# Turning a spectrum for the row transform: 90 TensorE transposes, or VectorE's 32x32 blocks of overlapping row ranges

## The chip, the cores and the metric

The kernel runs on one core of a Trainium2 chip. The metric is the device time of one execution in microseconds (us), the median of several runs; lower is better. All arithmetic is fp32.

A core has engines that each work through a queue of their own, in order: TensorE (PE in the profile; PEld is its loading of weights), VectorE (DVE), ScalarE (ACT), GpSimd (POOL) and SyncE (SP, which here only starts DMA transfers). They wait for each other by semaphores. TensorE writes into PSUM, and what is needed again is copied from there into SBUF.

## The reference

The input x is 8 images of 8 channels of 256 x 256. A Fourier neural operator in 4 groups runs on the normalized image, then a 3x3 dilation follows. Cut to what matters:

```python
h = _gconv1x1(h, fc0_w, fc0_b)                 # 4 groups x 10 channels
for i in range(4):
    h1 = _spectral_conv(h, sp_w1[i], sp_w2[i]) # rfft2, keep 24 x 12 modes, mix 10x10 channels, irfft2
    h2 = _gconv1x1(h, w_w[i], w_b[i])
    h = h1 + h2
    if i < 3:
        h = _gswish(h, betas[i])
h = _gswish(_gconv1x1(h, fc1_w, fc1_b), betas[3])   # 4 x 128 hidden channels
return _gconv1x1(h, fc2_w, fc2_b)
...
x = x + conv(gn(x)); x = x + dilate3x3(gn(x))
```

Only 12 modes along the width and 24 along the height are kept, so the kernel does the transforms as matrix products: first along the width (256 columns to 12 complex modes), then along the rows (256 rows to 24 modes).

## The kernel before, in words

**Staging.** One image's state `h` (40 channels of 256 x 256) stays in SBUF for all four layers. Its free dimension is cut into 11 chunks (`NCH`); every chunk has two rows for each of 4 x 3 sets (`NQ` quarters and `NBLK` blocks). The 30 channel-and-block rows of a group or of a quarter, with two spare ones, lie in 32 partitions.

**A layer** (`layer`, L423) goes through the chunks. `burst` (L469) multiplies the state by the layer's weights (L479) and adds the inverse transform of the mixed spectrum (L482, which reads `zt`); ScalarE's Silu puts the result back into `h` (L488). In layers 0 to 2 the forward transform for the next layer is made at the same time: `turn` (L426) transposes the new state in 32x32 blocks on VectorE (L430), `transform` multiplies by the cosine table along the width (L447) and `gather` (L453) adds the four partial sums by a matrix of identities (L461) and copies the sum, the spectrum along the width, into `zt` (L464, L467). `zt` has the shape [128, 22 rows, 4, 32]: after the bursts have read their part of the old contents, the new ones take their place. Before the change, the 128 partitions are 4 groups x 32 modes, and the third index runs over the quarters.

**Between two layers** `spectrum_h` (L312) takes the transform along the rows. For this the row index must lie in the partitions, so `zt` is turned first: for each of 30 columns, TensorE transposes a [128 x 88] slice (22 rows x 4 quarters) into PSUM (L320), eight of them into one PSUM tile `p_at`, and a copy (L195 on VectorE, in the first image every other one L193 on ScalarE) puts it into `turned`. Then 48 matrix products (L332), which the profile counts as 96 instructions, contract the rows with the table `eh_f` into `p_b`; six small products put the result into `bt`. `mix` (L352) multiplies by the spectral weights with 6 products (L359) and 6 sums (L362) on VectorE, `p_f` (L378) folds the result, and `rows_of` (L397) makes the inverse transform along the rows (`p_g`, L404 or L409) and writes it to `zt`. `spectrum_h` runs for layers 1, 2 and 3 of each image, 24 times in all.

**The head of the previous image.** The two last convolutions (`head`, L607) are done for the previous image beside the layers of the current one, in 128 steps. A step has a `first` (L627: 4 products with 512 columns into two PSUM tiles, two Silus of 1024 elements on ScalarE, L629) and, in every other step, a `second` (L649: 8 products into one PSUM tile, then an addition on VectorE, L652 or L654). The output of the dilation of the image before that (`dilate`) is woven in as well. For the first image there is no previous one; the last image's head runs alone at the end.

**The order of the work** is written out by hand: the instructions stand on each engine's queue in the order in which the program emits them. The generators of the layers yield numbers; `step()` emits one head step for each full unit of the running sum, where a number counts with a factor `scale` so chosen that the 128 steps are used up by the image's end:

```python
else:
    loose += n
    share += n * scale if scale else 0
    while share >= 1.0:
        share -= 1.0
        step()
scale = scale or (STEPS - exact) / loose
```

A tuple such as `(1,)` in the bursts stands for an exact number of steps, and `"even"` and `"odd"` add one where the count calls for it.

**PSUM** is one pool of four buffers of two banks, handed round in order of emission (`ps_z`). A `first` takes two, a `second` one, `p_at`, `p_b`, `p_f`, `p_g` one each.

The functions that the diff touches, and what calls them, as they stand before:

Of the kernel before, what the change touches and what calls it, by code (L numbers as in the profile page):

```python
# [20 lines left out]
G = 4  # L21
WID = 10
# [10 lines left out]
NBLK = 3  # L33
NCH = 11
NQ = 4
# [9 lines left out]
def fno_dilate_kernel(ctx: ExitStack, tc: tile.TileContext, a: dict, out: bass.AP):  # L45
# [28 lines left out]
    def load(name, shape, eng=nc.gpsimd):  # L74
        t = const.tile(list(shape), F32, tag=f"c_{name}", name=f"c_{name}")
        eng.dma_start(t, a[name])
        return t
# [20 lines left out]
    fold = load("fold", (128, 3, 32))  # L98
    rowg = load("rowg", (128, NBLK, NQ, CS))
    binv = load("binv", (128, HW))  # L100
    eh_f = load("eh_f", (CS * NQ, 3, NBLK, 32))
    bias3 = load("bias3", (128, 1))
    w1 = load("w1", (128, NBLK, HID))
    w2 = load("w2", (128, G, 47))
# [203 lines left out]
    def spectrum_table(k, term):  # L308

        return 0 if k == term else (1 if k == 0 else 2)  # L310

    def spectrum_h(b, l, out_):  # L312

        rows = turned.rearrange("p t f -> p (t f)")[: CS * NQ, : NBLK * WID * 128]
        view = rows.rearrange("p (i g k) -> p i g k", g=G, k=32)
        for j0 in range(0, NBLK * WID, 8):
            n = min(8, NBLK * WID - j0)
            t = ps_z(f"p_at_{b}_{l}_{j0}")
            for i in range(n):
                nc.tensor.transpose(  # L320
                    t[: CS * NQ, i // 4, 128 * (i % 4) : 128 * (i % 4 + 1)],
                    zt[:, :, :, j0 + i].rearrange("p r j -> p (r j)"), ident)
            copy(
                j0 // 8, rows[:, 128 * j0 : 128 * (j0 + n)], t[: CS * NQ].rearrange("p u w -> p (u w)")[:, : 128 * n])
            yield 0.6
        p = ps_a(f"p_b_{b}_{l}")
        for k in range(2):
            for n in range(2 * NBLK):
                term, blk = n // NBLK, n % NBLK
                for q in range(4):  # L330
                    k0 = 12 * term + 3 * q
                    mm(p[part(q), 120 * k : 120 * k + 120], eh_f[:, spectrum_table(k, term), blk, :],  # L332
                       view[:, WID * blk : WID * (blk + 1), :, k0 : k0 + 3],
                       start=n == 0, stop=n == 2 * NBLK - 1)
        bt = sb.tile([128, 2, 3, G, WID], F32, tag="B", bufs=1, name=f"B_{b}_{l}")
        s = io[:, 4 * l : 4 * l + 4]
        for part_ in range(2):
            for k in range(3):
                nc.vector.tensor_tensor(
                    bt[:, part_, k].rearrange("p g i -> p i g"),  # L340
                    p[:, 120 * part_ : 120 * part_ + 120].rearrange(
                        "p (i g k) -> p i g k", i=WID, g=G)[:, :, :, k],
                    s.unsqueeze(1).to_broadcast([128, WID, G]), ALU.mult,
                )
        out_["bt"] = bt
# [77 lines left out]
    def layer(b, l, out_, stored, side):  # L423
        group_in_f = l % 2 == 1

        def turn(c):  # L426

            dst = turned[:, c % 3].rearrange("p (s f x) -> p f s x", s=2, f=NQ)
            for i in range(2):
                nc.vector.transpose(  # L430
                    dst[:, 2 * i : 2 * i + 2], h[:, c, 2 * i : 2 * i + 2].rearrange("p f (s x) -> p f s x", s=2))

        def chunks_of(k):

            return sorted(range(2 * k, min(2 * k + 2, NCH)), key=lambda c: c % 3)

        def transform(k):


            cs = chunks_of(k)  # L440
            n, lo = len(cs), cs[0] % 3
            step = cs[-1] % 3 - lo if n == 2 else 1
            t = turned[:, lo : lo + step * (n - 1) + 1 : step].rearrange("p n (r v i) -> p n r v i", r=2 * NQ, v=8)
            pair = [ps_z(f"p_d_{b}_{l}_{k}_{i}") for i in range(2)]
            for v in range(8):
                for q in range(NQ):
                    mm(pair[q // 2][part(v % 4), q % 2, : 240 * n], fw8[part(q), v, :],  # L447
                       t[part(q), :, :, v, : NBLK * WID], start=v < 4, stop=v >= 4)
            e = turned[:, (2 * k + 1) % 3, : 960 * n].rearrange("p (q x) -> p q x", q=NQ)
            for i in range(2):  # L450
                copy_2(i, e[:, 2 * i : 2 * i + 2], pair[i][:, :, : 240 * n])

        def gather(k):  # L453

            cs = chunks_of(k)
            n = len(cs)
            e = turned[:, (2 * k + 1) % 3, : 960 * n].rearrange("p (q r f i) -> p q r f i", q=NQ, r=2 * n, f=NQ)
            p = ps_a(f"p_u_{b}_{l}_{k}")
            for g in range(G):
                m = e[:, g] if group_in_f else e[:, :, :, g].rearrange("p q r i -> p r q i")  # L460
                mm(p[part(g), : 240 * n], stack, m, start=True, stop=True)  # L461
            src = p[:, : 240 * n].rearrange("p (r j i) -> p r j i", r=2 * n, j=NQ)
            if cs == sorted(cs):
                nc.vector.tensor_copy(zt[:, 4 * k : 4 * k + 2 * n, :, : NBLK * WID], src)  # L464
            else:
                for i, c in enumerate(cs):
                    nc.vector.tensor_copy(zt[:, 2 * c : 2 * c + 2, :, : NBLK * WID], src[:, 2 * i : 2 * i + 2])  # L467

        def burst(c):  # L469
            pair = [ps_z(f"p_z_{b}_{l}_{c}_{i}") for i in range(2)]  # L470
            for f in range(NQ):
                for q in range(NQ):
                    o = pair[q // 2][part(f), q % 2, :]
                    if l == 0:
                        k = slice(32 * q, 32 * q + 6)
                        mm(o, wcn[k, :], h[k, c, f, :], start=True, stop=False)
                    else:
                        g = f if group_in_f else q
                        mm(o, wt[part(q), l, g, :], h[part(q), c, f, :], start=True, stop=False)  # L479
            for s in range(2):  # L480
                for q in range(NQ):
                    mm(pair[q // 2][:, q % 2, HW * s : HW * (s + 1)],  # L482
                       zt[part(q), 2 * c + s].rearrange("p f o -> p (f o)"), binv[part(q), :],
                       start=False, stop=s == 1)
            for i in range(2):
                dst = h[:, c, 2 * i : 2 * i + 2, :]
                if l < 3:
                    nc.scalar.activation(dst, pair[i], AF.Silu)  # L488
                else:
                    nc.scalar.activation(dst, pair[i], AF.Identity, bias=bias3)  # L490
            if l == 3:
                nc.sync.dma_start(stored[c], h[:, c].rearrange("p f w -> p (f w)"))

        def read_x(c):
            for g in range(G):
                nc.sync.dma_start(
                    h[32 * g : 32 * g + 6, c].rearrange("p f w -> p (f w)"), a["xp"][b, c, g])

        if l == 0:
            for c in range(NCH):  # L500
                read_x(c)
            wcn = sb.tile([128, 32], F32, tag="wcn", bufs=1, name=f"wcn_{b}")
            nc.vector.tensor_scalar(wcn, wc, out_["mr"][:, 1:2], None, ALU.mult)
        if l == 3:
            room = 0.0
            yield "odd"
            for c in range(NCH):
                burst(c)
                room += SIDE
                while room > 0.0:  # L510
                    room -= next(side, SIDE)
                yield (LAST,)
            return
        yield "even"
        for c in range(NCH):
            k = c // 2
            if c % 2 == 0:
                burst(c)
                yield (1,)
                turn(c)  # L520
                if k > 0:
                    transform(k - 1)
            else:
                burst(c)
                if k > 0:
                    gather(k - 1)
                yield (1,)
                turn(c)
        out_["sw"] = [load_sw(l + 1, 0), load_sw(l + 1, 1)]
        yield 1  # L530
        gather(k - 1)
        transform(k)
        yield 2
        gather(k)
        yield 1

# [251 lines left out]
def _tables():  # L788
# [17 lines left out]

    eh = np.where(real[None, ..., None], rows[:, row_of], 0.0).reshape(3, NBLK, NQ, CS, 32)
    eh = eh.transpose(2, 3, 0, 1, 4)

    line = np.linspace(0.0, 1.0, HW).astype(f32)  # L810

# [25 lines left out]
    for j, v in enumerate(planes):  # L837
# [8 lines left out]
    edge[:, 0], edge[:, 1] = np.where(top, -BIG, BIG), np.where(bottom, -BIG, BIG)  # L846
    edge[:, 2], edge[:, 3] = np.where(top, PAD, -BIG), np.where(bottom, PAD, -BIG)
    tables = {
        "fw": fw, "fw8": fw8, "stack": np.tile(np.eye(32), (4, 1)), "eh0": eh0, "eh_f": eh.transpose(1, 0, 2, 3, 4).reshape(CS * NQ, 3, NBLK, 32),
        "rowg": rowg.reshape(128, NBLK, NQ, CS),  # L850
        "fold": fold.reshape(128, 3, 32), "binv": binv.reshape(128, HW),
        "xe": xe.reshape(128, 6, G, 5), "grp": grp, "edge": edge,
# [68 lines left out]
```

## Time and profile before

| | before |
|---|---|
| time, median of 3 runs | 4109.72 us (4108.55 to 4111.58) |
| span of the profiled execution | 4109.4 us |
| mean granted clock of TensorE | 0.979 |
| TensorE busy | 93% |
| ScalarE busy | 70% |
| VectorE busy | 60% |
| head: L629 on ScalarE / L627 and L649 on TensorE | 1961.8 / 1201.7 and 996.9 us |
| L430, transposes of the state on VectorE | 622.9 us |

How to read it: a group of instructions is named by its line, engine and operation, then by what it writes and reads with the partitions and elements; after the count come the busy time of the group in us and the mean duration of one instruction in ns, then the idle time of the engine just before them and what ended it. For TensorE the busy time counts overlapping instructions once, so that busy time divided by count gives the pace, and the mean the time from start to end of one. Slices are fortieths of the span; a digit is the busy share in tenths. The first image takes up the time until about 400 us, the last head alone the time from about 3730 us.

### The profile page before, as it was taken

How to read it: one execution, taken by the hardware profiler on the slowest of the kernel's cores; microseconds unless marked ns; L12 is line 12 of the kernel's file. 1: busy time of each engine (PE TensorE's matmuls, PEld its weight loads, DVE VectorE, ACT ScalarE, POOL GpSimd, SP SyncE). 2: the span in 40 equal slices, each digit the busy share in tenths (PEclk: the TensorE clock that was granted, in tenths of full speed). 3: DMA queues.
4: the chain of work that ended last, by engine and by line, in shares of the span. 5: the costliest groups of instructions: out<-in, count | busy, mean ns of one | idle time of the engine just before them, and what ended most of it. 6: DMA issues, size and time to landing. Idle time of an engine off the chain costs nothing. (4 is left out here: it accounts for less than half of the span.)

```text
span 4109.4 us, 120095 instructions
## 1 busy us (share of the span) xinstructions
PE 3822.8 (93%) x54250; PEld 1529.8 (37%) x54250; DVE 2472.1 (60%) x3529; ACT 2860.1 (70%) x2997; POOL 117.0 (3%) x202
## 2 busy tenths in 40 slices
PE   5768999999999999999999999999999999999997
PEld 2434433333333343433333334343433433333222
DVE  6665565556566566665666666655676666663533
ACT  3436676776767777676777766777676776668887
POOL 1000000000000000000000000000000000000000
PEclk8988999999999999999999999999999999999998
DMA  2014111422125211261113511144121531215311
GB/s 83 14 46 157 56 42 33 163 88 64 57 75 175 64 57 57 83 195 43 58 57 108 175 47 48 49 145 136 55 58 47 169 101 59 61 47 191 94 52 48
DMA packets 113991, 345.09 MB, mean 84 GB/s; under 512 B 15772, under 2 KB 18396, under 8 KB 98057
## 3 DMA queue, kind: packets, MB, share of 16 engines
q1 hardware_dynamic: 95288, 276.33, 21.5%
q0 software_dynamic: 18192, 61.08, 4.5%
q8 instruction: 427, 7.00, 0.7%
q14 instruction: 84, 0.68, 0.1%
HBM read 213.36 MB, written 123.74 MB: 82 GB/s over the span
## 5 line engine op out<-in xcount | busy, mean ns | idle before, releaser
L629 ACT ACTIVATE act<-p_fc 128x1024 f32<-128x1024 f32 x2048 | 1961.8, 1026 | 735.1 <-PE p_fc L627 730.8
L627 PE MATMUL p_fc<-hs,c_w 32*128 32x512 f32 x8192 | 1201.7, 632 | 14.6 <-issue 8.3
L649 PE MATMUL p_fc<-act,c_w 128*32 128x512 f32 x8192 | 996.9, 603 | 47.1 <-ACT act L629 35.5
L627 PEld LDWEIGHTS p_fc<-hs,c_w 32*128 32x128 f32 x8192 | 398.3, 183 | 690.0 <-ACT act L629 270.4
L488 ACT ACTIVATE h<-p_z 128x1024 f32<-128x1024 f32 x528 | 511.7, 1021 | 189.1 <-PE p_z L482 188.6
L430 DVE STREAM_TRANSPOSE turned<-h 128x1024 f32<-128x1024 f32 x528 | 622.9, 1219 | 20.2 <-ACT h L488 19.9
L654 DVE TENSOR_TENSOR y<-p_fc,y 128x512 f32<-128x512 f32 x392 | 271.0, 691 | 543.0 <-PE p_fc L649 541.6
L649 PEld LDWEIGHTS p_fc<-act,c_w 128*32 128x32 f32 x8192 | 222.1, 110 | 636.2 <-issue 349.3
L482 PE MATMUL p_z<-c_binv,zt 32*128 32x256 f32 x5632 | 411.1, 405 | 0.9 <-ACT zt L193 0.9
L479 PE MATMUL p_z<-h,c_wt 32*32 32x512 f32 x8448 | 371.3, 602 | 6.7 <-DVE y L652 3.8
L482 PEld LDWEIGHTS p_z<-c_binv,zt 32*128 32x128 f32 x5632 | 261.3, 186 | 306.2 <-issue 289.1
L447 PE MATMUL p_d<-turned,c_fw 32*32 32x480 f32 (+1 forms) x9216 | 310.6, 541 | 12.5 <-DVE turned L430 12.5
L195 DVE COPY zt<-p_g 128x264 f32<-128x264 f32 x300 | 162.4, 629 | 169.5 <-PE p_g L409 94.0
L490 ACT ACTIVATE h<-p_z,c_bias 128x1024 f32<-128x1024 f32 x176 | 186.5, 1110 | 48.1 <-PE p_z L482 47.8
L199 ACT ACTIVATE turned<-p_d 128x960 f32<-128x960 f32 x144 | 130.0, 903 | 97.4 <-PE p_d L447 97.4
L447 PEld LDWEIGHTS p_d<-turned,c_fw 32*32 32x32 f32 x9216 | 121.8, 103 | 188.9 <-issue 151.3
L362 DVE TENSOR_REDUCE S<-turned 128x80 f32<-128x800 f32 x192 | 188.9, 984 | 5.0
L359 DVE TENSOR_TENSOR turned<-t,B 128x800 f32<-128x800 f32 x192 | 188.5, 982 | 0.9 <-DMA t<-in_spw 0.9
L461 PE MATMUL p_u<-turned,c_stack 128*32 128x480 f32 (+1 forms) x1152 | 137.9, 548 | 45.1 <-DVE turned L201 43.0
L479 PEld LDWEIGHTS p_z<-h,c_wt 32*32 32x32 f32 x8448 | 94.3, 103 | 205.8 <-ACT act L629 68.3
L201 DVE COPY turned<-p_d 128x960 f32<-128x960 f32 x144 | 152.1, 1057 | 30.3 <-PE p_d L447 30.1
L195 DVE COPY turned<-p_at 88x1024 f32<-88x1024 f32 x90 | 101.7, 1155 | 75.8 <-PE p_at L320 70.7
(172 smaller groups left out, 2134.7 us busy)
## 6 DMA issues: line engine op xcount, KB each, us to landing
stored<-h SPq DMA_DIRECT2D x88, 1024.0 KB
hs<-stored SPq DMA_DIRECT2D x352, 256.0 KB
t<-in_spw SPq DMA_DIRECT2D x96, 400.0 KB
yin<-y_rows POOLq DMA_DIRECT2D x56, 512.0 KB, 4.8
h<-in_xp SPq DMA_DIRECT2D x352, 48.0 KB
turned<-in_x SPq DMA_DIRECT2D x16, 1024.0 KB
y<-in_x SPq DMA_DIRECT2D x56, 256.0 KB
y_rows<-y POOLq DMA_DIRECT2D x56, 256.0 KB, 2.3
```

Of the source, the lines that this page charges most:

```text
L195: nc.vector.tensor_copy(dst, src)
L359: nc.vector.tensor_tensor(pr, sw[k], bt[:, k2, k].unsqueeze(2).to_broadcast([128, G, 2 * WID, WID]), ALU.mult)
L362: nc.vector.tensor_reduce(s[k2][:, k].rearrange("p g s o -> p (g s o)"), pr.rearrange("p g m i -> p (g m) i"), AX.X, ALU.add,)
L430: nc.vector.transpose(dst[:, 2 * i : 2 * i + 2], h[:, c, 2 * i : 2 * i + 2].rearrange("p f (s x) -> p f s x", s=2))
L447: mm(pair[q // 2][part(v % 4), q % 2, : 240 * n], fw8[part(q), v, :], t[part(q), :, :, v, : NBLK * WID], start=v < 4, stop=v >= 4)
L479: mm(o, wt[part(q), l, g, :], h[part(q), c, f, :], start=True, stop=False)
L482: mm(pair[q // 2][:, q % 2, HW * s : HW * (s + 1)], zt[part(q), 2 * c + s].rearrange("p f o -> p (f o)"), binv[part(q), :], start=False, s ...
L488: nc.scalar.activation(dst, pair[i], AF.Silu)
L627: mm(pair[g // 2][:, g % 2, :], w1[part(g), blk, :], hs[k][part(g), :], start=True, stop=True)
L629: nc.scalar.activation(act[:, 2 * i : 2 * i + 2, :], pair[i], AF.Silu)
L649: mm(acc[part(g), :], w2[:, g, 15 - rb - i : 47 - rb - i], act[:, g, :], start=i == 0, stop=i == 1)
L654: nc.vector.tensor_tensor(y, sums, y, ALU.add)
```

## The change

The transform along the rows gets its turned spectrum from VectorE. VectorE can transpose 32x32 blocks, each within 32 partitions. For this `gather` now writes `zt` so that the 128 partitions are 4 quarters x 32 modes and the third index runs over the groups (it loops over the quarters in place of the groups). `spectrum_h` then transposes, in four instructions, one for each group, 30 blocks of 32 modes x 32 rows. A chunked quarter has only 22 rows, so a block takes rows 0 to 15 and rows 6 to 21 (`windows`): ten rows appear twice. The table `eh_f` has 128 rows in place of 88 and holds zeros for the second appearance. The matrix products into `p_b` keep their number and columns and contract 128 partitions. The PSUM tiles `p_at` and their copies are gone. In place of the four yields of 0.6 there are four of 1.2.

```diff
-    eh_f = load("eh_f", (CS * NQ, 3, NBLK, 32))
+    eh_f = load("eh_f", (128, 3, NBLK, 32))
...
+    def windows(g):
+
+        v = zt[:, 0:16, g, : NBLK * WID].rearrange("p r i -> p i r")
+        (pp, pn), (i0, i1), (r0, r1) = [tuple(x) for x in v.ap]
+        return bass.AP(v.tensor, v.offset, [[pp, pn], [i0, i1], [(CS - 16) * r0, 2], [r0, r1]])
+
     def spectrum_h(b, l, out_):
 
-        rows = turned.rearrange("p t f -> p (t f)")[: CS * NQ, : NBLK * WID * 128]
-        view = rows.rearrange("p (i g k) -> p i g k", g=G, k=32)
-        for j0 in range(0, NBLK * WID, 8):
-            n = min(8, NBLK * WID - j0)
-            t = ps_z(f"p_at_{b}_{l}_{j0}")
-            for i in range(n):
-                nc.tensor.transpose(
-                    t[: CS * NQ, i // 4, 128 * (i % 4) : 128 * (i % 4 + 1)],
-                    zt[:, :, :, j0 + i].rearrange("p r j -> p (r j)"), ident)
-            copy(
-                j0 // 8, rows[:, 128 * j0 : 128 * (j0 + n)], t[: CS * NQ].rearrange("p u w -> p (u w)")[:, : 128 * n])
-            yield 0.6
+        rows = turned.rearrange("p t f -> p (t f)")[:, : NBLK * WID * 128]
+        view = rows.rearrange("p (g i k) -> p i g k", g=G, k=32)
+        for g in range(G):
+
+            nc.vector.transpose(
+                rows[:, 960 * g : 960 * (g + 1)].rearrange("p (i r) -> p i r", r=32), windows(g))
+            yield 1.2
         p = ps_a(f"p_b_{b}_{l}")
...
-            for g in range(G):
-                m = e[:, g] if group_in_f else e[:, :, :, g].rearrange("p q r i -> p r q i")
+            for g in range(NQ):
+                m = e[:, :, :, g] if group_in_f else e[:, g].rearrange("p q r i -> p r q i")
                 mm(p[part(g), : 240 * n], stack, m, start=True, stop=True)
-            src = p[:, : 240 * n].rearrange("p (r j i) -> p r j i", r=2 * n, j=NQ)
+            src = p[:, : 240 * n].rearrange("p (r g i) -> p r g i", r=2 * n, g=G)
...
+    eh_f = np.zeros((NQ, 32, 3, NBLK, 32))
+    eh_f[:, :16], eh_f[:, 48 - CS :] = eh[:, :16], eh[:, 16:]
```

The title's 90 are the transposes of one image's three calls.

More of the change, by code (lines that the diff above doesn't have):

```diff
@@ L848, in _tables @@
     tables = {
-        "fw": fw, "fw8": fw8, "stack": np.tile(np.eye(32), (4, 1)), "eh0": eh0, "eh_f": eh.transpose(1, 0, 2, 3, 4).reshape(CS * NQ, 3, NBLK, 32),
+        "fw": fw, "fw8": fw8, "stack": np.tile(np.eye(32), (4, 1)), "eh0": eh0, "eh_f": eh_f.reshape(128, 3, NBLK, 32),
         "rowg": rowg.reshape(128, NBLK, NQ, CS),
```

## The prediction

> **What bounds the kernel now.** I read the page first, then the groups by line, the waits of TensorE, and the timeline of one place where the changed code runs. From the page:
>
> ```profile
> PE 3822.8 (93%) x54250; PEld 1529.8 (37%) x54250; DVE 2472.1 (60%) x3529; ACT 2860.1 (70%) x2997; POOL 117.0 (3%) x202
> ...
> PE   5768999999999999999999999999999999999997
> ```
>
> TensorE is busy in nine tenths or more of every slice between the first image (slices 1 to 4) and the end, and no other engine is over 70%. A busy TensorE can still hide waits, so I look at what the operations concerned cost:
>
> ```profile
> L430 DVE STREAM_TRANSPOSE turned<-h 128x1024 f32<-128x1024 f32 x528 | 622.9, 1219 | 20.2 <-ACT h L488 19.9
> ...
> L362 DVE TENSOR_REDUCE S<-turned 128x80 f32<-128x800 f32 x192 | 188.9, 984 | 5.0
> ...
> L195 DVE COPY turned<-p_at 88x1024 f32<-88x1024 f32 x90 | 101.7, 1155 | 75.8 <-PE p_at L320 70.7 <-ACT act L629 5.1
> L320 PE MATMUL p_at<-ident,zt 128*88 128x128 f32 x720 | 92.4, 278 | 1.6 <-DVE zt L464 1.6
> ...
> L332 PE MATMUL p_b<-turned,c_eh_f 88*32 88x120 f32 x2304 | 90.6, 293 | 3.2 <-DVE turned L195 3.2
> ...
> L195 DVE COPY turned<-p_xt 128x512 f32<-128x512 f32 x56 | 35.3, 684 | 41.1 <-PE p_xt L250 41.1
> ...
> L195 DVE COPY turned<-p_a 32x512 f32<-32x512 f32 x28 | 28.7, 1025 | 28.1 <-PE p_a L263 25.6 <-ACT turned L193 2.2
> ```
>
> The busy sum of L320 is 92.4 us: 3.85 us for each of the 24 calls of spectrum_h (8 images, 3 layers), 128 ns a transpose, although one lasts 278. They run back to back. The timeline of one interleaved call, start and duration first (lines of other engines left out):
>
> ```profile
> 2056.71 0.41 DVE L464 COPY zt<-p_u 128x240 f32<-128x240 f32 x1 [2.16 <-PE p_u L461]
> ...
> 2059.87 1.98 PE L320 MATMUL p_at<-ident,zt 128*88 128x128 f32 x16
> ...
> 2061.08 2.35 DVE L195 COPY turned<-p_at 88x1024 f32<-88x1024 f32 x2 [0.73 <-ACT act L629]
> ...
> 2068.98 3.12 PE L332 MATMUL p_b<-turned,c_eh_f 88*32 88x120 f32 x80 [0.35 <-DVE turned L195]
> ...
> 2074.95 2.01 PE L627 MATMUL p_fc<-hs,c_w 32*128 32x512 f32 x16
> 2075.09 0.69 DVE L654 TENSOR_TENSOR y<-p_fc,y 128x512 f32<-128x512 f32 x1 [0.28 <-PE p_fc L649]
> ...
> 2077.26 1.93 PE L649 MATMUL p_fc<-act,c_w 128*32 128x512 f32 x16 [0.30 <-ACT act L629]
> ```
>
> From 2056.9 to 2072.1 us (15.2 us) the windows give TensorE 14.81 busy, VectorE 6.88, ScalarE 7.64. So TensorE is what this stage lasts, with hardly a gap: the head steps of the previous image (first: 4 L627 matmuls, about 1.02 us of TensorE; second: L649, 1.92 us, then one VectorE add of 0.69) fill it between the transposes. In the mix after it a second and two firsts repeat every 4.17 us, of which 0.3 is TensorE waiting for ScalarE's Silu.
>
> **The Trainium skill.** "TensorE: Matmul & The Clock Gate", Part 4 (PE-mode transpose), says that a full transpose goes to PSUM and needs a copy after it, and that most of a transpose's recorded time is access latency; the trace agrees (278 ns recorded, 128 ns apart, and the copies L195). "Vector Engine (DVE) Microarchitecture Reference", section 3.8, says that the 32x32 transpose streams one element per cycle per lane; L430 shows 1219 ns for 1024 elements, 1.19 ns each with its start-up, and reads contiguously. "SBUF — State Buffer", Door 1 (the remark on cachelines), says that accesses which cross to a new 16-byte line each time pay a penalty. The new transposes read zt with 512 bytes between consecutive elements. No row of before has such a read on VectorE; strided writes do show a penalty (worked out below).
>
> **The change, part by part.**
>
> *Removed from TensorE:* 30 transposes per call, 3.85 us; per interleaved image 3 x 3.85 = 11.6 us. The p_b matmuls stay 96 of 120 columns; 128 rows in place of 88 and another order of strides I take as free, since runs of 3 elements are gathered in both. The four PSUM buffers of p_at go too.
>
> *VectorE:* three copies of 1.22 and one of 0.95 go (4.6 us), four transposes T of 960 elements come. Duration T, from both sides: at the rate of L430, (960/1024) x 1219 = 1.15 us. With the strided penalty: the copy of p_a (same 512 elements, written 64 bytes apart) takes 1025 against 684 ns for p_xt, 0.67 ns per element more, so T = 1.15 + 960 x 0.67 ns = 1.8 us. The upper bound is an access at half rate, about 1.15 + 1.0 = 2.15 us. I take 1.8: a read of the SBUF that touches a new line each time should be no cheaper than such a write. VectorE's total then rises by 24 x (7.2 - 4.6) = 62 us; at 60% busy the total costs nothing, but the place can.
>
> *Gather:* the loop over q in place of g exchanges which layers read e contiguously; the p_u matmuls take 1.01 us for 8 in either kind of layer, so nothing. The larger eh_f is loaded once.
>
> *Emission:* a call now yields 4 x 1.2 = 4.8 units instead of 2.4, so more of the previous image's 128 steps fall into it, and fewer elsewhere (the sum stays 128). The instruction order of the changed program gives, between the last p_u and p_b, 5, 6 and 6 firsts and 2, 3 and 3 seconds for the three layers, where before had 4, 3, 3 and 2, 2, 1. The mixes lose one or half a step each.
>
> *The wait that is left:* p_b must wait for the fourth T. Behind the T's in VectorE's queue stand the adds of the seconds, each of which waits for its L649 and releases a PSUM buffer. I walk through it with time 0 at the end of the last p_u, zt copied at 0.55, firsts and seconds at the pace 4.17 per pair:
> - first layer: T1 to 2.35; add and statistics of the second 3.05 to 4.45; T2, T3 to 8.05; add to 8.75; T4 to 10.55. TensorE has done its steps by about 9.4 (the last first waits for the buffer of that add). Wait: 1.2.
> - second layer: T1 2.35; add, statistics 4.45; T2 6.25; add about 7.8; T3, T4 to 11.4. TensorE is busy to about 12.4. Wait: 0.
> - third layer: add, statistics to 3.4; T1, T2 to 7.0; add 7.7; T3 9.5; add (its L649 ends at 10.3) to 11.05; T4 12.85, against 12.35. Wait: 0.5.
> That is about 1.8 us per image.
>
> *Lost besides:* the transposes filled the 0.27 us in which TensorE otherwise waits for ScalarE in each pair of steps; five pairs per image (those that stood among them) lose it: 1.3 us. In the mixes, with fewer steps, p_f now comes sooner after VectorE's last product; walking through the orders I find 0.9 us in one of the three mixes and little in the others: 1.0 us.
>
> *Net per interleaved image:* 11.6 - 1.8 - 1.3 - 1.0 = 7.5 us; seven such images: 52.5 us.
>
> *The first image* has no head steps beside it, so the chain is bare: zt copied at 119.73 us of the trace, p_b's main run at 123.95, 4.2 us. Now 4 x 1.8 + 0.1 = 7.3: 3.1 us longer, three times, 9.3 us slower.
>
> Sum: 4109.7 - 52.5 + 9.3 = 4066.5 us.
>
> **Rivals.**
> - *The strided read is free* (T = 1.15). No wait before p_b, 0.5 in the mixes: 7 x (11.6 - 1.3 - 0.5) = 68.6; first image + 0.3 to 0.5 each, 1.5. Time 4043. For it: the transposing array is said to sustain a cycle per element. Against it: the cost of strided writes.
> - *Slower transposes or more given back* (T = 2.15, waits 2.2 + 0 + 1.1 = 3.3, mixes 1.5): 7 x 5.5 = 38.5, first image 13.5: 4085. If mixes, p_g and p_u also return 5 us per image at T = 1.8, 7 x 3.5 - 9.3 = 15: 4094. For it: the mix keeps VectorE at 11.09 of 13.2 us. Against it: where before has the same order of steps ahead of p_f, waits at p_f are 0.7 us in 500.
> - *VectorE becomes the bound of the call, and it is slower.* It takes T near 3.2: the walks then end at 15.4, 15.4 and 17.6, waits 14.3 us per image, so 7 x (14.3 + 1.3 + 1.5 - 11.6) = 38 more, and 26 in the first image: 4174. For it: a long queue on an in-order engine with TensorE at its end. Against it: no strided row of before is over about 1.8 ns per element without start-up (p_g's copy: 629 ns for 264), where this needs 3.2.
> - *No change* needs T about 2.6 or a new hidden bound; ScalarE, at 70%, has room for steps that come 1% sooner.
>
> **How the numbers follow.** T = 1.8: 0.55; free stride: 0.22; slower or given back: 0.13; slower than before: 0.06; near no change: 0.04. The likeliest is 4066. The range goes from just under the free stride, 4037, to the larger give-back, 4095; what is left out is 0.1 to 0.2. Faster (under 4101.5): the first three cases less a part of the third's tail, 0.88; same 0.05; slower 0.07.
>
> **What would show it.** Right: L320 as a TensorE line gone (-92 us of busy TensorE), 96 new STREAM_TRANSPOSE with a mean near 1.8 us, p_b waiting for them 1 us in the first and third layers and none in the second, about 3 us more per call in the first image. A mean of 1.15 makes the time 4043; one over 2.6 makes the forecast wrong. If the mean is 1.8 and the gain still under 25 us, the fault lies in the redistribution of the head steps: then waits at p_f, p_g or p_u will have grown.

## The result, and the profile after

| | before | after |
|---|---|---|
| time, median | 4109.16 us (4 runs, 4108.55 to 4111.58) | 4048.69 us (4 runs, 4043.43 to 4052.02) |
| ratio to before, 95% interval | | 0.9851 [0.9834, 0.9868] |
| TensorE busy | 3822.8 us | 3734.7 us |
| VectorE busy | 2472.1 us | 2538.8 us |

The changed kernel is 60 us faster; 43 were forecast (4066, range 4037 to 4095). The profiled execution of after is the fastest of its four (span 4041.6). The lines of its page that answer to those of before, with line numbers now up to one higher:

```profile
PE 3734.7 (92%) x53530; PEld 1463.3 (36%) x53530; DVE 2538.8 (63%) x3535; ACT 2853.1 (71%) x2991; POOL 117.0 (3%) x202
...
PE   5666999999999999999999999999999999999997
...
L324 DVE STREAM_TRANSPOSE turned<-zt 128x960 f32<-128x960 f32 x96 | 175.6, 1857 | 0.6
```

TensorE has 88 us less to do, about the 92 us of the transposes, and behind the first image it still fills nearly every slice. The new transposes take 1.86 us each, against the 1.8 taken. TensorE's matmuls into p_b, from the groups by line of after:

```profile
L333 PE MATMUL p_b<-turned,c_eh_f 128*32 128x120 f32 x2304 | 93.1, 306 | 32.2 <-DVE turned L324 24.8 <-issue 7.4
```

Before, the idle time ahead of this group was 3.2 us; now it is 32.2. So the change bought 92 us of TensorE for 29 us of waiting. Where these waits lie is seen in two places. First a call beside head steps, in the timeline of TensorE and then of VectorE (start and duration first):

```profile
2030.38 0.61 PE L462 MATMUL p_u<-turned,c_stack 128*32 128x240 f32 x8
...
2038.70 2.07 PE L628 MATMUL p_fc<-hs,c_w 32*128 32x512 f32 x16
2041.01 1.92 PE L650 MATMUL p_fc<-act,c_w 128*32 128x512 f32 x16 [0.24 <-ACT act L630]
2042.86 1.14 PE L628 MATMUL p_fc<-hs,c_w 32*128 32x512 f32 x8
2043.93 3.73 PE L333 MATMUL p_b<-turned,c_eh_f 128*32 128x120 f32 x96
```

VectorE in the same stretch:

```profile
2031.50 1.88 DVE L324 STREAM_TRANSPOSE turned<-zt 128x960 f32<-128x960 f32 x1
...
2036.01 1.86 DVE L324 STREAM_TRANSPOSE turned<-zt 128x960 f32<-128x960 f32 x1
...
2039.50 3.63 DVE L324 STREAM_TRANSPOSE turned<-zt 128x960 f32<-128x960 f32 x2
```

The fourth transpose ends at 2043.1, and p_b starts at 2043.9 without a wait: the head steps between cover it. Now the first image's first call, where there are no steps:

```profile
119.54 0.41 DVE L465 COPY zt<-p_u 128x240 f32<-128x240 f32 x1 [0.74 <-PE p_u L462]
119.98 6.80 DVE L324 STREAM_TRANSPOSE turned<-zt 128x960 f32<-128x960 f32 x4
...
126.88 4.58 PE L333 MATMUL p_b<-turned,c_eh_f 128*32 128x120 f32 x96 [7.41 <-issue]
```

TensorE idles 7.4 us, and p_b takes 4.58 us instead of 3.73. Three such calls are 22 us of the 32.2. The other 10 are 0.7 us ahead of p_b in the first and in the third call of each of the seven interleaved images; their second calls, of which the one above is an example, have no such wait.

The starts of p_b divide the span by image. From the third image's first call to the eighth's, five images took 2470.9 us before and 2413.5 after: 11.5 us less per image. The end of the third p_b, where the first image's losses are complete, moved from 291.2 to 304.3 us: 13.1 us lost. 7 x 11.5 - 13.1 = 67, the difference of the two spans (67.8).

TensorE's waits in those five images before the change (sum in us, times, longest):

```profile
PE p_fc L649 <- ACT act L629: 14.3, 50, 0.3
...
PE p_f L378 <- ACT act L629: 3.7, 15, 0.3
...
PE p_b L332 <- DVE turned L195: 1.7, 5, 0.3
```

The same after it:

```profile
PE p_fc L650 <- ACT act L630: 14.5, 51, 0.3
PE p_b L333 <- DVE turned L324: 7.8, 11, 0.7
...
PE p_f L379 <- ACT act L630: 2.8, 10, 0.3
```

Of these only the wait for p_b has grown much. One of its eleven waits ends where the stretch begins; the ten inside are 7.1 us, 1.1 us per image more than before. The waits for Silu and ahead of p_f, for which the prediction had taken off 2.3 us per image, changed by 0.2 us up and 0.9 down in all five.

### The profile page after: what moved, and what is told of

It reads as the page before. It is cut to its first block, busy times and chain, and to the rows that moved or that the text cites. A ratio compares the mean times of both kernels' runs of the same rounds, so it can differ in the third digit from the quotient of the medians.

```text
span 4041.6 us, 118640 instructions
## 1 busy us (share of the span) xinstructions
PE 3734.7 (92%) x53530; PEld 1463.3 (36%) x53530; DVE 2538.8 (63%) x3535; ACT 2853.1 (71%) x2991; POOL 117.0 (3%) x202
## 4 chain that ended last, share of the span: by engine, by line
PE 78%; DVE 11%; ACT 7%; issue 3%; DMA 1%; POOL 0%; DVEq 0%; POOLq 0%; SPq 0%; ACTq 0%
PE p_fc L650 22%; PE p_fc L628 20%; PE p_z L483 8%; PE p_z L480 7%; PE p_d L448 6%; ACT act L630 4%; PE p_u L462 3%; PE p_z L477 3%; DVE turned L431 2%; PE p_b L333 2%; PE p_g L405 2%; PE p_g L410 2%; ACT h L491 2%; DVE turned L324 2%; DVE turned L201 1%
## 5 line engine op out<-in xcount | busy, mean ns | idle before, releaser
L650 PE MATMUL p_fc<-act,c_w 128*32 128x512 f32 x8192 | 997.5, 601 | 47.1 <-ACT act L630 35.5
L483 PE MATMUL p_z<-c_binv,zt 32*128 32x256 f32 x5632 | 411.7, 405 | 0.6 <-ACT zt L193 0.6
L483 PEld LDWEIGHTS p_z<-c_binv,zt 32*128 32x128 f32 x5632 | 261.6, 186 | 305.4 <-issue 295.8
L462 PE MATMUL p_u<-turned,c_stack 128*32 128x480 f32 (+1 forms) x1152 | 137.3, 546 | 42.9 <-DVE turned L201 42.9
L324 DVE STREAM_TRANSPOSE turned<-zt 128x960 f32<-128x960 f32 x96 | 175.6, 1857 | 0.6
```

Source lines behind the costliest of these rows:

```text
L324: nc.vector.transpose(rows[:, 960 * g : 960 * (g + 1)].rearrange("p (i r) -> p i r", r=32), windows(g))
L483: mm(pair[q // 2][:, q % 2, HW * s : HW * (s + 1)], zt[part(q), 2 * c + s].rearrange("p f o -> p (f o)"), binv[part(q), :], start=False, s ...
L650: mm(acc[part(g), :], w2[:, g, 15 - rb - i : 47 - rb - i], act[:, g, :], start=i == 0, stop=i == 1)
```

## The experiments

Each was timed in rounds with the kernel before on the same chip. The theory is that the gain is TensorE's transposes gone, less the waits for the fourth transpose, which head steps cover where there are any. The rivals: the new spread of head steps is itself the gain; or the stride has no part in the 1.86 us; or VectorE's 37% of idle time would absorb any transpose.

**The spread of the steps alone.** The kernel before with the yields of after:

```diff
-            yield 0.6
+            yield 1.2
```

> The kernel before with the changed kernel's yields (1.2 in place of 0.6 in spectrum_h), so its head steps are spread as in the changed kernel, and TensorE still transposes. Theory 1 (the gain is TensorE's transposes gone; the spread only moves steps): within 6 us of before, near 4109. Theory 2 (the new spread of the steps is itself a gain, some 1.3 us an image or more): 4095 or less.

Measured: 4109.30 us, ratio 0.9996 [0.9988, 1.0005]. The spread alone brings nothing. The waits moved all the same (groups by line of this run; before had 1.6 us ahead of L320 and 35.5 us for Silu ahead of L649):

```profile
L649 PE MATMUL p_fc<-act,c_w 128*32 128x512 f32 x8192 | 1000.1, 602 | 38.6 <-ACT act L629 27.0 <-ACT h L490 10.6
...
L320 PE MATMUL p_at<-ident,zt 128*88 128x128 f32 x720 | 98.9, 281 | 9.1 <-DVE zt L464 5.3 <-ACT act L629 3.8
```

Transposes between steps do hide Silu waits, 8.5 us of them, but the transposes wait longer themselves.

**The yields alone undone.** The changed kernel with 0.6:

```diff
-            yield 1.2
+            yield 0.6
```

> The changed kernel with the yields of before (0.6 in place of 1.2). Theory 1 (the head steps of the call are what covers the transposes): with 4, 3, 3 firsts and 2, 2, 1 seconds TensorE is done 2 to 5 us before the fourth transpose, about 9 us more of waits for p_b in an image, 7 x 9 = 63 us: near 4110, the whole gain gone. Theory 2 (the yields do not matter): near 4049.

Measured: 4106.97 us, 0.9994 [0.9987, 1.0000]. The gain is gone. In the waits of this run p_b waits 71.1 us for L324, in 23 places. One call, from the timeline, and the same place by windows (us of the stretch; its length; busy time of TensorE, weight loads, VectorE, ScalarE and GpSimd; granted clock; DMA share and GB/s):

```profile
2070.95 1.80 DVE L324 STREAM_TRANSPOSE turned<-zt 128x960 f32<-128x960 f32 x1
...
2072.90 5.03 PE L333 MATMUL p_b<-turned,c_eh_f 128*32 128x120 f32 x96 [3.97 <-DVE turned L324]
```

The windows of the wait and of p_b:

```profile
2068.90:2072.90 4.00, 0.03 (x5) 0.03 (x2) 3.85 (x3) 1.94 (x2) 0.00 (x0) 0.87 0.32 93
2072.90:2077.90 5.00, 5.00 (x100) 4.64 (x100) 0.00 (x0) 0.00 (x0) 0.00 (x0) 0.50 0.01 3
```

The steps run out 4 us before the fourth transpose is done. And the gap costs more than itself: the granted clock (the third figure from the end) falls to 0.50, and p_b takes 5.0 instead of 3.7 us. Over the whole run the waits for p_b grew by 46 us, 6.6 per interleaved image where 9 were expected, and p_b's own time by 11.6 us, which the expectation had not counted. So its 4110 came out in part through a cost that it did not have.

**More steps in the call.** The changed kernel with 1.5:

> The changed kernel with yields of 1.5 in place of 1.2, so one more step stands in each call. Theory 1 (the waits that are left for p_b beside head steps are 1.4 us an image): they go, and the mixes, now shorter on TensorE than on VectorE, wait for about as much: 4040 to 4055. Theory 2 (more cover is free): 4038 or less.

Measured: 4056.43 us, 0.9867 [0.9852, 0.9882]: no better than 1.2, and by the medians worse, though the intervals of the two overlap. It lies 1.4 us above the range of the first theory. From its waits:

```profile
PE p_fc L650 <- ACT act L630: 40.2, 145, 0.6
PE p_b L333 <- DVE turned L324: 19.8, 9, 7.5
PE p_f L379 <- ACT act L630: 16.5, 14, 1.2
```

Against after the wait for p_b falls by 5 us, those ahead of p_f rise from 3.9 to 16.5 and those for Silu from 35.5 to 40.2. The loss in the mixes that the prediction expected of 1.2 sets in here: 1.2 still leaves the mixes enough steps.

**The stride taken away.** The transposes read 960 neighbours, so the row transform is taken of other elements:

```diff
-                rows[:, 960 * g : 960 * (g + 1)].rearrange("p (i r) -> p i r", r=32), windows(g))
+                rows[:, 960 * g : 960 * (g + 1)].rearrange("p (i r) -> p i r", r=32),
+                zt.rearrange("p r f o -> p (r f o)")[:, 600 * g : 600 * g + 960].rearrange("p (i r) -> p i r", r=32))
```

> The changed kernel, but its four transposes of a call read 960 neighbouring elements of zt in place of rows 512 bytes apart (so the row transform is taken of other data; the work is otherwise the same). Theory 1 (the stride costs 0.7 us of each transpose, and it reaches the time through the matmuls of p_b): the transposes fall from 1.86 to 1.15 us, p_b waits almost nowhere beside head steps (-1.4 us an image, 7 images), the first image gains 3 x (4 x 0.7), about 8 us: about 18 us faster than the changed kernel, near 4030. Theory 2 (the 1.86 us is the price of these transposes whatever they read): duration and time stay, near 4049.

Measured: 4030.00 us, 0.9803 [0.9788, 0.9817]. From the groups by line:

```profile
L324 DVE STREAM_TRANSPOSE turned<-zt 128x960 f32<-128x960 f32 x96 | 108.7, 1156 | 0.0
...
L334 PE MATMUL p_b<-turned,c_eh_f 128*32 128x120 f32 x2304 | 93.1, 307 | 18.2 <-DVE turned L324 9.8 <-issue 4.8 <-ACT act L631 3.6
```

0.70 us of each transpose are the stride's, and they cost 19 us of time. What is left ahead of p_b is mostly the first image (9.8 + 4.8 us).

**Each transpose twice.**

> The changed kernel with each transpose done twice, to the same place. Theory 1 (little room is left on VectorE at this place; the head steps cover just the four transposes): three calls of an interleaved image wait about 6, 4 and 5 us more, 7 x 15 = 105 us, the first image 3 x 7 = 21 us: near 4170, slower than before. Theory 2 (VectorE is busy 63%, the rest absorbs it): only the first image's 21 us show, near 4070.

Measured: 4210.87 us, 1.0242 [1.0226, 1.0257]; slower than before, and 40 us beyond what was expected. From the waits:

```profile
PE p_b L334 <- DVE turned L325: 81.6, 22, 14.8
PE p_fc L629 <- DVE y L654: 49.9, 19, 3.8
```

And p_b among the groups by line:

```profile
L334 PE MATMUL p_b<-turned,c_eh_f 128*32 128x120 f32 x2304 | 104.8, 347 | 98.5 <-DVE turned L325 81.6 <-issue 14.7 <-ACT act L631 2.1
```

The direction is that of the first theory, its sum is not. The waits for p_b rose from 32.2 to 98.5 us, by 66 where the expectation had 126. Two things it had left out. A second's addition stands behind a transpose in VectorE's queue, holds its PSUM buffer, and the firsts wait for that (the 49.9 us). And TensorE is busy 55 us longer with the same work, 12 of them in p_b (104.8 us for 93.1), at a mean granted clock of 0.961 for 0.977; how much of the 55 is the clock was not tried. VectorE is busy 64% here; its idle time elsewhere is of no use to the call.

**A layout that reads densely: rows innermost.**

```diff
-    zt = const.tile([128, CS, NQ, 32], F32, tag="zt", name="zt")
+    zt = const.tile([128, NQ, 32, CS], F32, tag="zt", name="zt").rearrange("p f o r -> p r f o")
```

> The changed kernel with zt stored as [128, 4, 32, 22], rows innermost, so that the transposes read neighbours and the result is whole again. The price is moved: the weights of L483 (zt for the bursts) are then read 88 bytes apart, the gather's copies write in steps of 88 bytes, while the copies out of p_g write densely. Theory 1 (the loads of weights run ahead of the matmuls and hide it): transposes 1.15 us and a time like that of the dense read, near 4030. Theory 2 (a strided load costs its 46 ns pace 1.7 times, 79 ns against 73 of a matmul, and gathers delay p_b): the gain is given back, 4050 to 4070.

Measured: 4119.41 us, 1.0027 [1.0018, 1.0037]. Slower than before, and more than the second theory had allowed for:

```profile
L483 PE MATMUL p_z<-c_binv,zt 32*128 32x256 f32 x5632 | 485.2, 458 | 0.1
...
L483 PEld LDWEIGHTS p_z<-c_binv,zt 32*128 32x128 f32 x5632 | 376.0, 330 | 300.1 <-issue 297.7 <-ACT zt L193 1.7
...
L324 DVE STREAM_TRANSPOSE turned<-zt 128x960 f32<-128x960 f32 x96 | 108.9, 1158 | 0.6
```

The transposes are as fast as they should be. But the weights of L483, loaded from zt at steps of 88 bytes, take 330 instead of 186 ns, and the products with them 73 us more of TensorE (485.2 against 411.7): 86 ns apiece for 73, where the second theory had 79. With fewer steps in the call:

> The same with yields of 0.9 in place of 1.2: four transposes now take 4.6 us and fewer steps cover them, the mixes keep more. Theory 1 (it is enough that the steps cover the transposes): within 5 us of the one with 1.2. Theory 2 (each call loses what it loses in steps, as in the changed kernel with 0.6): 15 us or more slower.

Measured: 4117.60 us, 1.0022 [1.0012, 1.0031], the same: the first theory.

**Two rows side by side.** zt as [128, chunk, 4, 32, 2], so that both readers use two neighbours of a line:

```diff
+    zs = const.tile([128, 16, NQ, 32, 2], F32, tag="zt", name="zt")
+    zt = zs.rearrange("p c f o s -> p c s f o")
+    fz = zs[:, NCH:].rearrange("p c f o s -> p (c f o s)").rearrange("p (o g k) -> p o g k", g=G, k=32)
...
+        return zs[:, :, g, : NBLK * WID, :].rearrange("p c i s -> p i c s")
...
-                copy(u, dst, src)
+                for s in range(2):
+                    copy(u, dst[:, :, :, :, s], src[:, :, :, :, s])
...
+    eh_f[:, :CS] = eh
```

> The changed kernel with zt stored as [128, 16, 4, 32, 2]: the two rows of a chunk lie side by side, so a transpose reads two neighbours before it jumps, and the weights of L483 are read 8 bytes apart (all of every line is used). A block takes 16 pairs, 11 of zt and 5 of fz, which lies behind it and meets zeros of the table. The copies into zt are cut in two (one for each row of a pair, one for each chunk). Theory 1 (the penalty is for an access that never uses its line twice): transposes near 1.2 us, weight loads stay at 186 ns, and it is 8 to 20 us faster than the changed kernel (4030 to 4040), the added copies costing a few us. Theory 2 (any step over one element costs): transposes near 1.5 us or more, weight loads over 250 ns, and it is slower than the changed kernel.

and the changed kernel beside it:

> The changed kernel once more, beside the run above on the same chip, as the measure for it: 4049 within 6 us.

Measured: 4033.51 us, 0.9815 [0.9802, 0.9828], against 4047.93, 0.9848 [0.9834, 0.9861] for the changed kernel in the same runs: 14 us faster, with intervals apart. It is the best of the study with the whole computation.

```profile
L479 PE MATMUL p_z<-c_binv,zt 32*128 32x256 f32 x5632 | 414.3, 407 | 0.3 <-ACT zt L193 0.2
...
L479 PEld LDWEIGHTS p_z<-c_binv,zt 32*128 32x128 f32 x5632 | 269.7, 193 | 300.5 <-issue 294.8 <-ACT zt L193 3.0
...
L322 DVE STREAM_TRANSPOSE turned<-zt 128x960 f32<-128x960 f32 x96 | 108.9, 1158 | 0.6
```

With two neighbours per line the transposes are as fast as dense ones, and the weight loads take 193 ns. With yields of 1.0:

> The kernel with the row pairs side by side and yields of 1.0 in place of 1.2: four transposes take 4.6 us now and need less cover. Theory 1 (once the transposes are covered, steps moved between the call and the mix change nothing): 4033 within 5 us. Theory 2 (the mixes gain from each step that comes back): 4025 or less.

Measured: 4034.88 us, 0.9822 [0.9808, 0.9835]: nothing more, the first theory.

**The clock of the first image.** In the first image, 52 transposes that nobody reads fill TensorE's gap:

```diff
+        if alone[0]:
+            t = ps_z(f"p_warm_{b}_{l}")
+            for i in range(52):
+                nc.tensor.transpose(t[:, 0, :128], ident, ident)
         p = ps_a(f"p_b_{b}_{l}")
```

> The changed kernel; in the first image alone TensorE makes 52 transposes of the identity into a PSUM tile that nobody reads, while VectorE turns the spectrum (6.7 us of idle filled). Theory 1 (a part of the first image's loss is the clock that TensorE is granted after the gap: p_b takes 4.6 to 5.0 us there at a clock near 0.66, 3.7 beside head steps): p_b back at about 3.8 us in the first image, 3 us in all off the time, 4045. Theory 2 (the slower p_b comes from bare access to turned, without other work): p_b stays at 4.6 to 5.0 us, time 4048.

```profile
118.77 5.90 PE L330 MATMUL p_warm<-ident 128*128 128x128 f32 x52
126.50 3.73 PE L337 MATMUL p_b<-turned,c_eh_f 128*32 128x120 f32 x96 [1.82 <-issue]
```

The windows of the first p_b, in the changed kernel and then here:

```profile
127.00:131.50 4.50, 4.47 (x96) 4.09 (x95) 0.00 (x0) 0.00 (x0) 0.00 (x0) 0.67 0.02 4
...
126.80:131.00 4.20, 3.43 (x95) 2.88 (x84) 0.70 (x7) 0.00 (x0) 0.00 (x0) 1.00 0.01 4
```

With the gap filled the granted clock is 1.00 instead of 0.67, p_b is back at 3.73 us, and the third p_b ends at 301.1 instead of 304.3 us: the clock was the cause, for 3.2 us. The whole time, 4048.30 us (4041.18 to 4053.01), does not show 3 us, since the runs of one kernel scatter by more; that part of the expectation can't be told.

## Why the prediction was right

- *What bounds it.* Right. TensorE lost 88 us of busy time and the kernel followed. That the spread of the steps alone brings nothing is shown (before with 1.2).
- *The duration T.* Right: 1.86 us for 1.8, of which 0.70 is the stride (0.65 taken), shown by the dense read (1.156 for 1.15). The estimate from the strided write of p_a was good to a few per cent. The Trainium skill, "SBUF — State Buffer", Door 1, says that two hits per line are needed for full bandwidth; the row pairs agree (1158 ns, against 1156 for neighbours). The rival of the free stride gave 4043 for T = 1.15; with T so, 4030 was measured, for the reason of the next points. By its time alone, 4049, the change lies nearer to this rival than to the likeliest case, 4066; the duration of the transposes tells them apart.
- *The wait for p_b beside head steps.* Right in kind and nearly in size: 1.8 us per image forecast (1.2, 0 and 0.5 in the three calls), 1.4 measured (0.7, 0 and 0.7). That it is the steps which cover the transposes is shown from both sides (0.6: gain gone; transposes twice: slower than before).
- *"Lost besides", 1.3 + 1.0 us per image.* This term was wrong: in sum it measured zero, which is 7 x 2.3 = 16 us of the forecast. For the 1.3, the instruction order had shown that more pairs of steps stand bare in the call. They do: by the timelines of the five images the waits for Silu ahead of seconds rose in the calls from 5 to 20, by 0.8 us per image. It had not been counted that these steps came out of the mixes, where they stood just as bare: there the waits fell from 45 to 31, by 0.8 us per image too. For the 1.0, the waits ahead of p_f fell from 3.7 to 2.8 us in five images; the prediction gives only the outcome of its walk through the mixes, so what in it was too hard on VectorE stays open. It is a real loss a step further on (yields of 1.5: 3.9 to 16.5 us).
- *The first image.* Right in kind, too small: 9.3 us forecast, 13.1 measured. The transposes behaved (6.8 us for the four, against 7.2 forecast); left out was that p_b after a gap of 7 us runs at a lower clock, 4.6 to 5.0 us for 3.7, which costs about 3 us in three calls (shown by filling the gap). The Trainium skill, "TensorE: Matmul & The Clock Gate", Why this matters for your kernels, warns of gaps over about 3 us between matmuls; the trace shows the clock at 0.50 behind one of 4.
- *The gather and eh_f.* Nothing, as forecast: the p_u matmuls took 137.9 us in all and take 137.3. 128 partitions in place of 88 are free in p_b too: 3.7 us a call beside head steps before and after.

The image's account from the trace: TensorE's busy time fell by 11.9 us (forecast 11.6), its waits rose by 0.4 (forecast 4.1). Of the 3.7 between, 2.3 are the term "lost besides", 0.7 the wait for p_b, which grew by 1.1 and not 1.8, and the rest small waits that fell, ahead of p_u, p_f and p_g. Together 11.5, not 7.5; 28 us more over seven images, less 3.8 in the first. The medians differ by 7 us less than the profiled executions, since the profiled one of after was 5 us under its median and that of before 2 us over.

## What to carry to other kernels

Moving work off the engine that bounds a stage paid nearly in full here, because the other engine's new work lay behind other work of the first. How much must lie there can be walked through in the queues, and giving too little (0.6) lost the whole gain. When such a move changes which instructions stand side by side, count the waits over the whole loop, not only where they newly appear: here the steps that moved took their waits along. For a layout with two readers, look for one in which both find two neighbours side by side before paying for a stride at either; here it gained 14 us, and the stride at the other reader lost 71.

## What the runs showed of the hardware that had not been expected

- Weight loads of TensorE pay for strides too: 186 ns dense, 193 at 8-byte steps, 330 at 88-byte steps (L483, L479). The products with them went from 73 to 86 ns apiece at 88 bytes.
- A gap of 4 us in TensorE's work halved the granted clock for the 5 us that followed (yields of 0.6), so that p_b took 5.0 us instead of 3.7. In the first image it was 0.67 over the first p_b behind a gap of 7.4 us. Transposes alone, 52 in 5.9 us, kept it at 1.00.
- A copy from PSUM that writes at 88-byte steps takes 1.23 us for 480 elements a partition, where the write in runs of 30 neighbours took 0.66 (gather, rows innermost and after).
